# Graph attention and dilated SAGE: scores in sixteen 32x32 array tiles, and running counts over pairs of columns

## The chip, the core and the metric

The kernel runs on one core of one Trainium2 chip. The time is that of the device in microseconds (us), from one launch; before the change the median of 3 runs is 3443.05 us (3439.62 to 3444.79). In the profile, PE is TensorE's matmuls, PEld its weight loads, DVE is VectorE, ACT ScalarE, POOL GpSimd and SP the engine that starts most DMAs.

## What is computed

The input is `x` (16 graphs of 1024 nodes with 128 features) and a weighted adjacency `adj` (16 x 1024 x 1024). There are two layers, each on a layer-normed, rectified `x`, each added to `x`. The first is attention with 8 heads of 16 features, masked by the edges and weighted by them:

```python
scores = einsum('bhnd,bhmd->bhnm', q, k) / math.sqrt(HD)
scores = where(adj == 0, -inf, scores)
attn = softmax(scores) * adj
attn = attn / (attn.sum(-1) + 1e-08)
ctx = einsum('bhnm,bhmd->bhnd', attn, v)      # then @ Wo.T + bo
```

The second first "dilates" the edges, node by node, since what an earlier node removes changes the counts of the later ones:

```python
row = carry[n]; num = sum(row)
sf = where(num > 10, (num + 1) // 2, 1)
rank = cumsum(row)
rm = row & (rank % sf == 0)                   # if valid and num > 1
carry[n] = row & ~rm; carry[:, n] = carry[:, n] & ~rm
```

With what is left of `adj`, three SAGE layers follow (neighbour means, two products, normalised rows, batch norm), and one product of all three.

## The kernel before

All lines are those of the profile. The work has two parts in time. In the first, attention runs over `turns` (L180): 16 graphs b, 2 halves c of the query nodes, 8 blocks m of 128 key nodes, and in each turn two groups g of four heads. That is 512 attention steps. Beside them, in the same instruction streams, runs the dilation, over 8 blocks k of 128 nodes for all 16 graphs at once. In the second part the SAGE layers run.

The order on TensorE, ScalarE and VectorE is the order in which the program is written out (the schedule is manual for these three engines, L1197). An attention step (L572 to L608) issues: the scores of its group; small pieces of other graphs' preparation; the value products of the step before (`late`); two exps on ScalarE (L590); two multiplications by the edge weights on VectorE (L595). Every second step also turns over a block of edges (`turn_over`, L489): four transposes, a copy, and the mask of missing edges, `nomask`, which is kept in four versions, version r rotated by 32r partitions (L507 to L509).

`scores` (L531) fills four PSUM banks, one for each head j of the group, held as two tiles `scs` of two banks each. First, 16 bfloat16 matmuls (L546) put -1e30 where an edge is missing; each uses one 32x32 tile of the array, and for one j the four row strips r all write bank j, in four different quarters of its partitions. Then four float32 matmuls (L552), one for each head, add the scores: 32 rows (the group's head j lies in row strip j, the other heads of the strip being zeroed in `qT`) by all 128 columns. The exps read the two tiles of `scs`, and the next step's scores are written to the same four banks.

`values` (L476) multiplies the weights by `v1`, 32 columns for each head: 16 values, a one (for the sum of the weights) and 15 zeros, in 128x32 array tiles (L479); with `eps8` it adds 1e-8 of the plain softmax sum (L484). The two buffers of `v1` for alternate graphs share one tile under the tag `aT2`.

The dilation of a block (`dilation`, L643) is a generator whose yields give an estimated cost and when it may go on: 0 at once, 1 in the next attention step, "A" or "B" in the next even or odd one. `beside_attention` (L936) takes pieces from it while the estimated cost spent is below the share of steps done. For a block it first finds which nodes of the block remove each other: counts inside the block (`w`, scanned at L747, shifted by 1024 and masked by `valid` at L785), seven rounds of comparing and counting (L799 to L841), and the block's final counts. Then come the block's rows, graph by graph (L889 to L933): a running sum along the row of 1024 nodes. The scan at L893 adds each node's edge and that of the node before, so that it yields the doubled count less a shift; ScalarE takes the absolute distance to a middle (`mid_at`, L906); VectorE compares it with `off` and keeps the edges to be removed (L910 to L915); eight transposes turn it (L900), ScalarE copies it (L902), and DMAs write both. In the same loop ScalarE reads the next block's edges (`read`, L691 and L695) and VectorE drops those already removed (`survive`, L708).

Of the kernel before, what the change touches and what calls it, by code (L numbers as in the profile page):

```python
# [10 lines left out]
F32 = mybir.dt.float32  # L11
# [10 lines left out]
P = 128  # L22
# [12 lines left out]
def swept(ctx: ExitStack, tc: tile.TileContext, t: dict, out: bass.AP, flag: bass.AP):  # L35
# [131 lines left out]
    def first_part(p1):  # L167
# [73 lines left out]

        v1_both = shared.tile([P, 2, NB, H, 32], F32, name="v1_both", tag="aT2")
        v1s = [v1_both[:, i] for i in range(2)]
        for v1 in v1s:
            nc.vector.memset(v1[:, :, :, HD:], 0.0)
            nc.vector.memset(v1[:, :, :, HD : HD + 1], 1.0)
        never = one.tile([P, P], BF, name="never")
# [37 lines left out]
        def prepare(b):  # L285
# [35 lines left out]
            def value(c, bank=(ps_m, "m")):  # L321
                pv = bank[0].tile([P, HB, D], F32, name=f"pv_{b}_{c}", tag=bank[1])
                start_with(pv, 0)
                for i in range(HB):
                    n = (c * HB + i) * P
                    nc.tensor.matmul(
                        pv[:, i, :], hT[:, n : n + P], wts["Wv"], start=False, stop=(i == HB - 1)
                    )
                yield "evict"
                nc.scalar.copy(  # L330
                    v1[:, c * HB : (c + 1) * HB, :, :HD], pv.rearrange("p k (h d) -> p k h d", d=HD)
                )
# [139 lines left out]
        def attention():  # L472
# [3 lines left out]
            def values(acc, v1, m, g, es, ws):  # L476

                for j in range(4):
                    nc.tensor.matmul(  # L479
                        acc[g][32 * j : 32 * j + 32, :], v1[:, m, 2 * j + g, :],  # L480
                        ws[j // 2][:, j % 2, :], start=(m == 0), stop=False,
# [49 lines left out]
            def scores(i, g):  # L531
# [5 lines left out]
                nomask = tiles[i][1]  # L537
                mm = slice(m * P, (m + 1) * P)
                scs = [
                    ps_s.tile([P, 2, HN], F32, name=f"sc_{b}_{c}_{m}_{g}_{q}", tag="sc")  # L540
                    for q in range(2)
                ]
                for j in range(4):
                    for r in range(4):
                        rows, to = slice(32 * r, 32 * r + 32), 32 * ((r + j) % 4)
                        nc.tensor.matmul(  # L546
                            scs[j // 2][to : to + 32, j % 2, :], never[rows, rows], nomask[rows, j, :],
                            start=True, stop=False, tile_position=(32 * r, to),
                        )
                for j in range(4):  # L550
                    rows = slice(32 * j, 32 * j + 32)
                    nc.tensor.matmul(  # L552
                        scs[j // 2][:, j % 2, :], kT[rows, mm], qTs[c][rows, g, :],
                        start=False, stop=True, tile_position=(32 * j, 0),
                    )
                made["of"], made["scores"] = (i, g), scs
# [86 lines left out]
        def dilation():  # L643
# [84 lines left out]
            for k in range(NB):  # L728
# [5 lines left out]

                up = shared.tile([P, B, P], BF, name=f"up_{k}", tag="mr", bufs=4)

# [3 lines left out]
                for dg, hb in zip(dgs, halves):  # L740
                    nc.vector.tensor_tensor(up[:, hb, :], dg, each_half(upto), ALU.mult)
                next(late, None)
                yield 1.3, 1
# [16 lines left out]
                for c, hb in enumerate(halves):  # L760
# [3 lines left out]
                    if c == 0:  # L764
                        nc.vector.tensor_copy(onw, w[:, :, P - 1])
                        for dg, of in zip(dgs, halves):
# [17 lines left out]

                nc.vector.scalar_tensor_tensor(  # L785
                    w.rearrange("p b i -> p (b i)"), w.rearrange("p b i -> p (b i)"), 1024.0,
                    valid.rearrange("p b i -> p (b i)"), ALU.add, ALU.mult,
                )
                yield 2.3, 1
                final = shared.tile([P, B, P], BF, name=f"final_{k}", tag="mr", bufs=4)  # L790
# [53 lines left out]

                th = small.tile([P, 4, B], F32, name=f"th_{k}", tag="th", bufs=2)
                num, mid_at, off, allof = (th[:, i, :] for i in range(4))
                high = v[:, 3, :]
# [7 lines left out]
                nc.vector.tensor_scalar(num, num, MAGIC, MAGIC, ALU.add, ALU.subtract)  # L855
                nc.vector.tensor_scalar(mid_at, num, -3.0, 1024.0, ALU.mult, ALU.add)
                nc.vector.scalar_tensor_tensor(off, num, 1.0, high, ALU.add, ALU.mult)
# [31 lines left out]
                for i in range(B + 2):  # L889
                    b = i  # L890
                    if b < B:
                        wrs[b] = pool.tile([P, N], F16, name=f"wr_{k}_{b}", tag="wr", bufs=2)
                        nc.vector.tensor_tensor_scan(  # L893
                            wrs[b], rk(b, 1, N + 1), rk(b, 2, N + 2), -1023.0, ALU.add, ALU.add
                        )
                    b = i - 2
                    if 0 <= b:
# [4 lines left out]
                        nc.scalar.copy(ets[b], pe)  # L902
                    yield (2.4 if i < B else 0.0), "B"
                    b = i
                    if b < B:
                        nc.scalar.activation(wrs[b], wrs[b], AF.Abs, bias=mid_at[:, b : b + 1])  # L906
                    b = i - 1
# [28 lines left out]
        def beside_attention():  # L936

            block = 1.3 + 4.6 + 3.9 + 1.4 + 1.2 + 3.6 + ROUNDS * 2.5 + 2.0 + 5.1 + 1.4 + B * 5.3 + 2.4
            total = B * 0.3 + NB * block
# [1023 lines left out]
```

## Time and profile before

| what | value |
|---|---|
| median of 3 runs | 3443.05 us |
| the profiled execution, its own time | 3445.77 us |
| its span, first to last instruction | 3443.9 us |
| mean granted TensorE clock | 0.994 |
| the first part (attention and dilation) ends at | about 2355 us |
| matmuls in 0 to 2355 us | 25771 |
| exps (L590) | 1024 x 1020 ns |
| edge multiplications (L595) | 1024 x 1217 ns |
| scans of rows (L893) | 128 x 2278 ns |

A row of the profile's groups reads: line, engine, operation, output <- inputs, partitions x elements and type of each, count | busy time in us, mean ns of one | idle time of the engine just before, and what ended it. Times by stage give, for each stretch of the span, its length, then the busy time of each engine with its number of instructions, the granted clock, the share of DMA and its rate. A timeline row gives the start, the time covered, the engine, the line and how many instructions are merged in it.

### The profile page before, as it was taken

How to read it: one execution, taken by the hardware profiler on the slowest of the kernel's cores; microseconds unless marked ns; L12 is line 12 of the kernel's file. 1: busy time of each engine (PE TensorE's matmuls, PEld its weight loads, DVE VectorE, ACT ScalarE, POOL GpSimd, SP SyncE). 2: the span in 40 equal slices, each digit the busy share in tenths (PEclk: the TensorE clock that was granted, in tenths of full speed). 3: DMA queues.
4: the chain of work that ended last, by engine and by line, in shares of the span. 5: the costliest groups of instructions: out<-in, count | busy, mean ns of one | idle time of the engine just before them, and what ended most of it. 6: DMA issues, size and time to landing. Idle time of an engine off the chain costs nothing. (4 is left out here: it accounts for less than half of the span.)

```text
span 3443.9 us, 86074 instructions
## 1 busy us (share of the span) xinstructions
PE 3364.4 (98%) x34855; PEld 1882.4 (55%) x34855; DVE 3096.0 (90%) x5255; ACT 2287.3 (66%) x3781; POOL 174.4 (5%) x253
## 2 busy tenths in 40 slices
PE   8999999999999999999999999999999899999997
PEld 3333333333333333333334334336999899999997
DVE  7899999889989999998998999997888799988887
ACT  7699689779879869968876986884322344423234
POOL 2000000000000000000000000000000000000000
PEclk9999999999999999999999999999999999999999
DMA  7356457547637746745763773677999799989996
GB/s 238 107 171 197 137 148 200 153 129 222 187 117 213 213 124 182 227 142 157 228 191 121 229 236 120 185 218 248 345 334 337 271 354 353 350 309 350 356 352 222
DMA packets 650121, 772.27 MB, mean 224 GB/s; under 512 B 173264, under 2 KB 569168, under 8 KB 637424
## 3 DMA queue, kind: packets, MB, share of 16 engines
q1 hardware_dynamic: 632672, 708.58, 63.7%
q0 software_dynamic: 15456, 57.30, 4.9%
q8 instruction: 275, 4.51, 0.6%
q14 instruction: 134, 1.10, 0.1%
q10 hardware_dynamic: 1584, 0.79, 0.1%
HBM read 508.50 MB, written 157.29 MB: 193 GB/s over the span
## 5 line engine op out<-in xcount | busy, mean ns | idle before, releaser
L595 DVE TENSOR_TENSOR w<-e,aT 128x1024 f32<-128x1024 f32 x1024 | 1203.9, 1217 | 107.9 <-ACT e L590 107.4
L590 ACT ACTIVATE e<-sc 128x1024 f32<-128x1024 f32 x1024 | 990.4, 1020 | 341.7 <-PE sc L552 340.6
L1117 PE MATMUL pg<-y,aT 128*128 128x128 f32 (+1 forms) x6144 | 732.2, 275 | 0.0
L1117 PEld LDWEIGHTS pg<-y,aT 128*128 128x128 f32 x6144 | 710.3, 192 | 0.0
L479 PE MATMUL acc<-w,v_both 128*32 128x512 f32 x4096 | 637.2, 605 | 6.9 <-DVE w L595 3.8
L484 PE MATMUL acc<-e,eps 128*32 128x512 f32 x4096 | 617.3, 593 | 0.0
L552 PE MATMUL sc<-qT,kT 32*128 32x512 f32 x4096 | 584.3, 640 | 0.3 <-ACT qT L308 0.3
L146 DVE SCALAR_TENSOR_TENSOR aT<-mr,aT 128x1024 f32<-128x1024 bf16 x384 | 458.8, 1217 | 0.0
L484 PEld LDWEIGHTS acc<-e,eps 128*32 128x32 f32 x4096 | 159.1, 110 | 294.6 <-issue 286.0
L1140 ACT ACTIVATE sq<-o 128x512 f32<-128x512 f32 x96 | 60.6, 631 | 358.1 <-DVE o L1135 358.1
L893 DVE TENSOR_TENSOR_SCAN wr<-rk 128x1024 f16<-128x1024 bf16 x128 | 291.6, 2278 | 0.0
L546 PEld LDWEIGHTS <-never 32*32 32x32 bf16 x8192 | 79.1, 88 | 340.4 <-issue 317.6
L546 PE MATMUL sc<-nomask,never 32*32 32x512 bf16 x8192 | 249.2, 385 | 11.0 <-ACT e L590 7.5
L1158 ACT COPY hT<-pt 128x512 f32<-128x512 f32 x96 | 56.2, 585 | 267.7 <-PE pt L1154 259.3
L552 PEld LDWEIGHTS sc<-qT,kT 32*128 32x128 f32 x4096 | 160.1, 183 | 116.9 <-issue 116.1
L479 PEld LDWEIGHTS acc<-w,v_both 128*32 128x32 f32 x4096 | 100.7, 108 | 203.6 <-DVE w L595 105.0
L497 PEld LDWEIGHTS pa<-ident,a 128*128 128x128 f32 x1024 | 108.1, 141 | 181.7 <-issue 134.2
L906 ACT ACTIVATE wr<-wr,th 128x1024 f16<-128x1024 f16 x128 | 148.0, 1156 | 46.8 <-DVE wr L893 45.8
L497 PE MATMUL pa<-ident,a 128*128 128x128 f32 x1024 | 168.8, 288 | 6.8 <-DMA a<-in_adj 6.1
L504 ACT ACTIVATE nomask<-aT 128x512 bf16<-128x512 f32 x256 | 161.4, 630 | 8.1
L1135 DVE SCALAR_TENSOR_TENSOR o<-pg,rdeg,mine 128x128 f32<-128x128 f32 x384 | 108.1, 344 | 60.4 <-PE pg L1117 56.8
L500 ACT COPY aT<-pa 128x512 f32<-128x512 f32 x256 | 151.6, 592 | 4.7 <-PE pa L497 4.7
(226 smaller groups left out, 3844.5 us busy)
## 6 DMA issues: line engine op xcount, KB each, us to landing
aT<-aT_d SPq DMA_DIRECT2D x94, 2048.0 KB, 9.8
mr<-mr_d SPq DMA_DIRECT2D x188, 512.0 KB, 6.1
aT_d<-aT SPq DMA_DIRECT2D x256, 256.0 KB, 4.1
a<-in_adj SPq DMA_DIRECT2D x253, 256.0 KB, 4.1
ad<-in_adj SPq DMA_DIRECT2D x112, 512.0 KB, 4.2
nomask<-nomask SPq DMA_DIRECT2D x512, 96.0 KB, 2.7
nomask<-nomask SPq DMA_DIRECT2D x512, 64.0 KB, 2.7
nomask<-nomask SPq DMA_DIRECT2D x512, 32.0 KB, 2.8
```

What stands on the lines that cost most here:

```text
L146: nc.vector.scalar_tensor_tensor(part, mrs[h][:, j : j + 2, :].rearrange("p j n -> p (j n)"), 0.0, part, ALU.is_equal, ALU.mult)
L479: nc.tensor.matmul(acc[g][32 * j : 32 * j + 32, :], v1[:, m, 2 * j + g, :], ws[j // 2][:, j % 2, :], start=(m == 0), stop=False,)
L484: nc.tensor.matmul(acc[g][32 * j : 32 * j + 32, :], eps8, es[j // 2][:, j % 2, :], start=False, stop=(m == NB - 1),)
L497: nc.tensor.transpose(pa[:, k * P : (k + 1) * P], a[:, k, :], ident)
L500: nc.scalar.copy(aT[:, 0, :], pa)
L504: nc.scalar.activation(nomask[:, 0, :], aT[:, 0, :], AF.Relu, bias=1.0, scale=-1e38, accum_out=zeros[:, i : i + 1])
L546: nc.tensor.matmul(scs[j // 2][to : to + 32, j % 2, :], never[rows, rows], nomask[rows, j, :], start=True, stop=False, tile_position=(32 * ...
L552: nc.tensor.matmul(scs[j // 2][:, j % 2, :], kT[rows, mm], qTs[c][rows, g, :], start=False, stop=True, tile_position=(32 * j, 0),)
L590: nc.scalar.activation(e, scs[q], AF.Exp, scale=1.0 / math.sqrt(HD))
L595: nc.vector.tensor_tensor(w, es[q], aT.to_broadcast([P, 2, HN]), ALU.mult)
L893: nc.vector.tensor_tensor_scan(wrs[b], rk(b, 1, N + 1), rk(b, 2, N + 2), -1023.0, ALU.add, ALU.add)
L1117: nc.tensor.matmul(pg[:, i // 2, at : at + width], aT[:, j, i * P : (i + 1) * P], y[:, j, :width], start=(j == 0), stop=(j == NB - 1),)
```

## The change

It has two halves.

The scores: a group's four float32 products become sixteen, each in a 32x32 tile of the array: head j stays in row strip j, and its 128 key columns go to four column tiles. The loops run with the rotation q outside and the row strip j inside, and row strip j writes column tile (q + j) mod 4 of bank j. The masks are rewritten in the same order, so that a row strip's mask goes to its own bank.

The counts: the scan of a row runs over 513 pairs of neighbouring columns in place of 1024 columns, and gives the plain count at the end of each pair, in float16. ScalarE then makes both columns of a pair from it, with a scale of 2 and two biases, writing every second element: from sum i for the even column and from sum i + 1 for the odd. The two buffers of pair sums lie in the tile of the value weights, which now stand 17 apart for each head (the 32 columns of a load run into the next head's; the rows of `acc` that come of it are not read). In the block's own counts, 1024 is put into the first column before the scan, so the later step is a multiplication alone. The estimated costs of the pieces are set to match.

```diff
-        v1_both = shared.tile([P, 2, NB, H, 32], F32, name="v1_both", tag="aT2")
-        v1s = [v1_both[:, i] for i in range(2)]
+        HW = HD + 1
+        VW = H * HW + 16
+        both = shared.tile([P, 4096], F32, name="both", tag="aT2")
+        v1s = [both[:, i * NB * VW : (i + 1) * NB * VW].rearrange("p (m w) -> p m w", w=VW) for i in range(2)]
...
+        free = 2 * NB * VW
+        pair_sums = [
+            both[:, free + i * (HN // 2 + 1) : free + (i + 1) * (HN // 2 + 1)].bitcast(F16)[:, : HN + 1]
+            for i in range(2)
+        ]
...
-                        acc[g][32 * j : 32 * j + 32, :], v1[:, m, 2 * j + g, :],
+                        acc[g][32 * j : 32 * j + 32, :], v1[:, m, (2 * j + g) * HW : (2 * j + g) * HW + 32],
...
-                for j in range(4):
-                    for r in range(4):
-                        rows, to = slice(32 * r, 32 * r + 32), 32 * ((r + j) % 4)
+                for q in range(4):
+                    for j in range(4):
+                        rows, to = slice(32 * j, 32 * j + 32), 32 * ((q + j) % 4)
                         nc.tensor.matmul(
-                            scs[j // 2][to : to + 32, j % 2, :], never[rows, rows], nomask[rows, j, :],
-                            start=True, stop=False, tile_position=(32 * r, to),
+                            scs[j // 2][to : to + 32, j % 2, :], never[rows, rows], nomask[rows, q, :],
+                            start=True, stop=False, tile_position=(32 * j, to),
                         )
-                for j in range(4):
-                    rows = slice(32 * j, 32 * j + 32)
-                    nc.tensor.matmul(
-                        scs[j // 2][:, j % 2, :], kT[rows, mm], qTs[c][rows, g, :],
-                        start=False, stop=True, tile_position=(32 * j, 0),
-                    )
+                for q in range(4):
+                    for j in range(4):
+                        rows, to = slice(32 * j, 32 * j + 32), 32 * ((q + j) % 4)
+                        nc.tensor.matmul(
+                            scs[j // 2][to : to + 32, j % 2, :],
+                            kT[rows, m * P + to : m * P + to + 32], qTs[c][rows, g, :],
+                            start=False, stop=True, tile_position=(32 * j, to),
+                        )
...
-                up = shared.tile([P, B, P], BF, name=f"up_{k}", tag="mr", bufs=4)
+                up = shared.tile([P, B, P], F16, name=f"up_{k}", tag="mr", bufs=4)
...
+                nc.vector.tensor_scalar(up[:, :, 0:1], up[:, :, 0:1], 1024.0, None, ALU.add)
...
-                nc.vector.scalar_tensor_tensor(
-                    w.rearrange("p b i -> p (b i)"), w.rearrange("p b i -> p (b i)"), 1024.0,
-                    valid.rearrange("p b i -> p (b i)"), ALU.add, ALU.mult,
-                )
-                yield 2.3, 1
+                nc.vector.tensor_tensor(w, w, valid, ALU.mult)
+                yield 1.3, 1
...
-                nc.vector.tensor_scalar(mid_at, num, -3.0, 1024.0, ALU.mult, ALU.add)
+                nc.vector.tensor_scalar(at_odd, num, -3.0, None, ALU.mult)
+                nc.vector.tensor_scalar(at_even, num, -3.0, 2.0, ALU.mult, ALU.add)
...
-                        wrs[b] = pool.tile([P, N], F16, name=f"wr_{k}_{b}", tag="wr", bufs=2)
+                        row = rk(b, 0, N + 2)
                         nc.vector.tensor_tensor_scan(
-                            wrs[b], rk(b, 1, N + 1), rk(b, 2, N + 2), -1023.0, ALU.add, ALU.add
+                            pair_sums[b % 2], row[:, 0::2], row[:, 1::2], 0.0, ALU.add, ALU.add
                         )
...
-                    yield (2.4 if i < B else 0.0), "B"
+                    yield (1.3 if i < B else 0.0), "B"
...
-                        nc.scalar.activation(wrs[b], wrs[b], AF.Abs, bias=mid_at[:, b : b + 1])
+                        wrs[b] = pool.tile([P, N], F16, name=f"wr_{k}_{b}", tag="wr", bufs=2)
+                        for t, at in enumerate((at_even, at_odd)):
+                            nc.scalar.activation(
+                                wrs[b][:, t::2], pair_sums[b % 2][:, t : t + HN], AF.Abs,
+                                bias=at[:, b : b + 1], scale=2.0,
+                            )
...
-            block = 1.3 + 4.6 + 3.9 + 1.4 + 1.2 + 3.6 + ROUNDS * 2.5 + 2.0 + 5.1 + 1.4 + B * 5.3 + 2.4
+            block = 1.3 + 4.6 + 3.9 + 1.4 + 1.2 + 2.6 + ROUNDS * 2.5 + 2.0 + 5.1 + 1.4 + B * 4.2 + 2.4
```

More of the change, by code (lines that the diff above doesn't have):

```diff
@@ L239, in node_masks @@
             )
-        v1_both = shared.tile([P, 2, NB, H, 32], F32, name="v1_both", tag="aT2")
-        v1s = [v1_both[:, i] for i in range(2)]
+        HW = HD + 1
+        VW = H * HW + 16
+        both = shared.tile([P, 4096], F32, name="both", tag="aT2")
+        v1s = [both[:, i * NB * VW : (i + 1) * NB * VW].rearrange("p (m w) -> p m w", w=VW) for i in range(2)]
         for v1 in v1s:
-            nc.vector.memset(v1[:, :, :, HD:], 0.0)
-            nc.vector.memset(v1[:, :, :, HD : HD + 1], 1.0)
+            nc.vector.memset(v1[:, :, H * HW :], 0.0)
+            nc.vector.memset(v1[:, :, HD : H * HW : HW], 1.0)
+        free = 2 * NB * VW
[3 more added lines that the diff above has]
+        ]
         never = one.tile([P, P], BF, name="never")
@@ L330, in value @@
                 nc.scalar.copy(
-                    v1[:, c * HB : (c + 1) * HB, :, :HD], pv.rearrange("p k (h d) -> p k h d", d=HD)
+                    v1[:, c * HB : (c + 1) * HB, : H * HW].rearrange("p k (h e) -> p k h e", e=HW)[:, :, :, :HD],
+                    pv.rearrange("p k (h d) -> p k h d", d=HD),
                 )
@@ L537, in scores @@
                 nomask = tiles[i][1]
-                mm = slice(m * P, (m + 1) * P)
                 scs = [
@@ L764, in dilation @@
                     if c == 0:
-                        nc.vector.tensor_copy(onw, w[:, :, P - 1])
+                        nc.vector.tensor_scalar(onw, w[:, :, P - 1], 1024.0, None, ALU.subtract)
                         for dg, of in zip(dgs, halves):
@@ L841, in dilation @@
                             nc.tensor.matmul(g, final[:, b, :], vb[:, 1, b, 0:1], start=False, stop=True)
-                th = small.tile([P, 4, B], F32, name=f"th_{k}", tag="th", bufs=2)
-                num, mid_at, off, allof = (th[:, i, :] for i in range(4))
+                th = small.tile([P, 5, B], F32, name=f"th_{k}", tag="th", bufs=2)
+                num, at_odd, off, allof, at_even = (th[:, i, :] for i in range(5))
                 high = v[:, 3, :]
```

## The prediction

> **What bounds the kernel now.** I read the page first, then busy time by stage, then the timeline of two attention steps, then the groups by form.
>
> The page's busy rows and its 40 slices:
>
> ```profile
> PE 3364.4 (98%) x34855; PEld 1882.4 (55%) x34855; DVE 3096.0 (90%) x5255; ACT 2287.3 (66%) x3781; POOL 174.4 (5%) x253
> ...
> PE   8999999999999999999999999999999899999997
> DVE  7899999889989999998998999997888799988887
> ACT  7699689779879869968876986884322344423234
> PEclk9999999999999999999999999999999999999999
> ```
>
> Attention with the dilation beside it fills some 27 slices (to about 2355 us, where the last L546 and L552 start); the SAGE layers fill the rest, and the change doesn't touch them. ScalarE's row swings in attention, eight times. So I cut that part at the first L893 scan of each block and 12 us after its last one: "row stages", where each block's 16 rows of counts are built (about 34 attention steps each), and "other stages" between them.
>
> ```profile
> core 0: us, PE busy (x) PEld busy (x) DVE busy (x) ACT busy (x) POOL busy (x), PEclk, DMA share, GB/s
> 177.51:325.58 148.07, 146.35 (x1574) 52.42 (x1574) 140.60 (x197) 143.25 (x234) 6.93 (x6) 1.00 0.64 183
> 325.58:453.15 127.57, 126.98 (x1526) 46.81 (x1510) 113.64 (x198) 90.72 (x142) 6.99 (x8) 1.00 0.46 140
> ...
> 1876.71:2038.55 161.84, 158.72 (x1589) 54.91 (x1580) 158.44 (x214) 142.68 (x207) 6.03 (x6) 1.00 0.77 225
> 2038.55:2169.45 130.90, 130.34 (x1683) 51.76 (x1667) 120.29 (x230) 89.72 (x136) 10.57 (x16) 1.00 0.47 142
> 2169.45:2317.07 147.62, 145.63 (x1580) 51.87 (x1576) 144.33 (x170) 125.69 (x170) 8.90 (x13) 1.00 0.69 207
> ```
>
> The other stages (second and fourth rows) are TensorE's: 99% busy, VectorE at 89 to 92%, ScalarE at 70%. The row stages are close to three bounds at once: in block 0 ScalarE is at 97%, VectorE at 95%; by block 6 VectorE is at 98% and ScalarE at 88%. All eight row stages last 148.07, 149.93, 151.63, 153.92, 157.00, 159.47, 161.84, 147.62; the last has no next block to read.
>
> A busy TensorE need not be at its peak, so I took the timeline of one step on it:
>
> ```profile
> 1001.88 0.43 PE L546 MATMUL sc<-nomask,never 32*32 32x512 bf16 x16
> 1002.25 1.14 PE L552 MATMUL sc<-qT,kT 32*128 32x512 f32 x8
> ...
> 1002.78 0.61 PE L552 MATMUL sc<-qT,kT 32*128 32x512 f32 x4
> 1003.32 0.66 PE L497 MATMUL pa<-ident,a 128*128 128x128 f32 x4
> 1003.91 1.07 PE L479 MATMUL acc<-w,v_both 128*32 128x512 f32 x8
> 1004.79 1.04 PE L484 MATMUL acc<-e,eps 128*32 128x512 f32 x8
> ```
>
> Each float32 product is two array passes (four products, eight instructions). L479 to L484 is 0.88: two passes of 0.43 and 0.03 for the first weights, with no seam, since both use 128x32 tiles. L552's first pass takes 0.53 (1002.25 to 1002.78), so 0.10 of it is the load of 128 weight columns; its second takes 0.54, so 0.11 is emptying the array before another shape. Masks and scores together: 0.37 + 1.07 = 1.44 us a step, 512 steps.
>
> **The scores.** Both groups now use 32x32 tiles. Gone are the emptying between L546 and L552 (0.11) and the exposed load (0.10): 32 columns load in 0.03 and can load while the masks stream. What stays: first load 0.03, mask pass 0.21 (an estimate: half of a float32 pass), two score passes 0.86, the spread of 16 starts 0.05 to 0.10, emptying 0.11. That is 1.26 to 1.31; I take 1.28, so 0.16 saved. From below: if the seam isn't a matter of shape, nothing is saved.
>
> It adds 24 matmuls and 24 weight loads a step. Row L546: 16 loads of 88 ns each cover 0.14 us, so starts are about 3.5 ns apart. Against the change speaks the Trainium skill, "TensorEngine Tiling (Array Packing)", section Instruction Overhead: about 60 cycles per matmul, which at the 2.4 GHz of its TensorE page is 25 ns. By it 24 more cost 0.6 us a step, 0.6 - 0.21 = +0.4 net. This trace has such a row too, but for full-array matmuls:
>
> ```profile
> 395.30 0.16 PE L840 MATMUL gone<-vb,valid 128*128 128x1 bf16 x1
> 395.33 0.16 PE L841 MATMUL gone<-vb,final 128*128 128x1 bf16 x1
> ```
>
> 25 ns apart, all in one array tile. L546 is the nearer row (same tiles, same 512 columns), and I go by it. Streaming four column tiles of float32 at once is L479's habit; four row strips at once is L552's.
>
> The same page (Gotcha 1) says that different row tiles can't use one PSUM bank at a time. Before, L546 wrote one bank from four row strips, in different quarters, and its 16 still took 0.37; after, each strip has its bank. By the rule the masks would gain; by the row they are already one pass. I count nothing.
>
> A wait moves: the first four masks now touch all four banks, so the first mask waits for both exps, where before eight masks went ahead of the second exp. Queued behind it on TensorE are all masks, the scores, then the previous step's values. But before, no score could start until the last eight masks had followed the second exp, so the exp-to-score distance is about one mask pass either way: 0 (at most +0.05).
>
> **The counts.** Rows by form:
>
> ```profile
> L893 DVE TENSOR_TENSOR_SCAN wr<-rk 128x1024 f16<-128x1024 bf16 x128 | 291.6, 2278 | 0.0
> L830 DVE TENSOR_TENSOR hit<-w,at 128x2048 bf16<-128x2048 f16 x56 | 68.2, 1218 | 0.5
> L785 DVE SCALAR_TENSOR_TENSOR w<-w,valid 128x2048 f16<-128x2048 f16 x8 | 18.2, 2274 | 0.0
> L504 ACT ACTIVATE nomask<-aT 128x512 bf16<-128x512 f32 x256 | 161.4, 630 | 8.1
> L906 ACT ACTIVATE wr<-wr,th 128x1024 f16<-128x1024 f16 x128 | 148.0, 1156 | 46.8 <-DVE wr L893 45.8
> ```
>
> - Scan: 2278 ns for 1024 steps is 2.22 ns a step; 513 steps are 1.14 us, up to 1.3 if the stride-2 reads cost. I take 1.17: 1.11 less a row, 17.8 a row stage, VectorE.
> - Abs: one pass over 1024 becomes two over 512. L504 is 630 for 512; a per-partition bias costs 0.1 (L906's 1156 against 1051 for L691's 1024 without one; L317's 512 with one takes 692). Two of 0.71, less the 0.10 by which the two exps of a step overlap (1.94 for two of 1.02), is 1.32 to 1.40: +0.16 to +0.25 (+0.3 if interleaved writes cost), I take 0.21, ScalarE: +3.4 a row stage.
> - L785 becomes a tensor_tensor of 2048 like L830: -1.05 a block; two added small VectorE instructions (175 ns, row L856) +0.35. This lies in the other stages, where VectorE waits anyway: 0; if VectorE were the bound there, -0.7 x 8 = -6.
> - The value weights at a stride of 17: the same 512 elements per copy (L330, 591 ns) and 32 columns per load: 0. The pair sums share a tile with them; if that made either wait for the other, the scan of row b+2 is a row (some 9 us) behind row b's Abs, and the value copy comes twice an image: 0, at worst 1 us an image.
> - The planner's costs shrink, but in the code a block has some 62 yields that demand a new attention step; 8 of them fill nearly all 512 steps. The dilation keeps its pace in steps: 0. No DMA, SP or POOL instruction is added or moved.
>
> **The sum.** Row stages, blocks 0 to 6: ScalarE's busy time is 143.25, 141.74, 144.31, 145.19, 145.09, 144.71, 142.68. VectorE falls to 123 to 141. TensorE needs at most the 145.6 of block 7's stage, which does the same work, less 34 x 0.16 = 5.4: 140. So ScalarE comes last. With 3.4 more each and 98% busy (block 0 has 97% with both others beside it), the stages take 149.6, 148.1, 150.7, 151.6, 151.5, 151.1, 149.1: 1051.7 against 1081.9, -30. Block 0's grows by 1.5. Block 7's, with ScalarE at 125.7 + 3.4 and VectorE at 126.6, follows TensorE: -5.5. Other stages: 512 - 8 x 34 = 240 steps x 0.16 = 38; VectorE, up from 90% to 93%, will hand some back (its L595 feeds L479), so nine tenths: -34. Total -69.5: 3445.8 of the profiled execution (its span 3443.9) becomes 3376; from the median 3443.05, 3374.
>
> **Rivals.**
> - *ScalarE takes more of it.* For: its 97% in block 0. With +0.3 per Abs and 96.7%: (1007.0 + 33.6)/0.967 = 1076, -6; other stages -25, block 7 -5: 3407. Beside it, *the seam stays* (the change doesn't do what it says on TensorE): only -30: 3413.
> - *Everything shrinks.* TensorE at 1.23 (0.2 saved, 240 steps: -48), ScalarE at 99.5% in row stages (-46), -7: 3342. Against: three engines would have to mesh better than now.
> - *Slower: TensorE can't start the pairs fast enough.* Behind the masks' wait for the second exp stand 16 + 32 load-and-matmul pairs. At L840's 25 ns the last pair starts at 1.20 and ends at 1.20 + 0.43 + 0.11 = 1.74, 0.30 over today. It decides from 48d + 0.54 = 1.44, d = 19 ns. Other stages +72; row stages 145.6 + 10.2 = 155.8 at 98.7%, 158 each, +35: 3550. For: that row and the skill's 60 cycles. Against: L546's 3.5 ns in these tiles.
>
> **Chances.** Likeliest 0.46 (3355 to 3395); everything shrinks 0.13; ScalarE 0.13; seam stays 0.06; gains and costs level out within 0.2%, about what a measurement of this kernel can tell from no change, 0.06; slower 0.16. Faster 0.78. The range goes from 3335 (the second case) over the level case to 3450, leaving out the slower one.
>
> **What would show it.** Right: from the first L546 to the group after L552 about 1.28 us in place of 1.44, with no gap between L546 and L552; L893 at 1.17 us; two L906 rows near 0.7 us; row stages near 150 us and level over the blocks, ScalarE 97 to 98% in them; other stages 4 to 5 us shorter. Wrong: score starts 25 ns apart, or second passes waiting for another column tile of their row strip (then five passes, 2.1 us); waits of L893 on TensorE, which would be the shared tile; a row stage that follows VectorE still.

## The result, and the profile after

The changed kernel takes 3462.15 us (median of 5 runs, 3457.27 to 3464.22) against 3442.01 for the kernel before beside it: ratio 1.0057, 95% interval 1.0042 to 1.0072. It is 0.6% slower, where 3374 was predicted. The profiled execution spans 3462.4 us, 18.5 more than before.

The page of the changed kernel, its busy row and two of its 40 slices:

```profile
PE 3360.8 (97%) x47143; PEld 1947.8 (56%) x47143; DVE 2968.8 (86%) x5271; ACT 2332.1 (67%) x3909; POOL 163.8 (5%) x253
...
DVE  7888988888889898988988999897888799988887
ACT  7699689779869968967976986894232344423334
```

VectorE lost 127 us of work, ScalarE gained 45, TensorE's busy time is nearly the same (3360.8 for 3364.4) with 12,288 more matmuls, and the span grew. So the work of the two fullest engines doesn't account for the new time; it has to be looked for in when things start. Busy time by stage of the changed kernel, cut as before (row stage and other stage of block 0; row stage 6, other stage, row stage 7):

```profile
core 0: us, PE busy (x) PEld busy (x) DVE busy (x) ACT busy (x) POOL busy (x), PEclk, DMA share, GB/s
176.18:326.58 150.40, 146.16 (x2326) 56.85 (x2326) 124.77 (x196) 148.65 (x250) 4.86 (x6) 1.00 0.61 178
326.58:458.06 131.48, 129.98 (x2250) 51.47 (x2246) 113.56 (x200) 91.32 (x142) 6.97 (x8) 1.00 0.47 140
1899.01:2051.64 152.63, 150.70 (x2353) 59.46 (x2333) 141.65 (x213) 146.94 (x222) 4.97 (x6) 1.00 0.76 227
2051.64:2190.71 139.07, 135.92 (x2410) 56.26 (x2403) 120.81 (x234) 90.50 (x137) 10.57 (x16) 1.00 0.49 148
2190.71:2335.63 144.92, 143.86 (x2384) 56.66 (x2368) 129.40 (x170) 131.65 (x186) 7.83 (x13) 1.00 0.71 214
```

The row stages look much as predicted: level at about 150 us, VectorE with room, ScalarE at 96 to 99% in the first seven. The eight last 150.4, 152.4, 151.2, 151.5, 152.9, 153.8, 152.6, 144.9, together 19.7 less than before, where 35.5 was predicted. The loss is in the other stages: 131.48 for 127.57, and 139.07 for 130.90. All other stages together, from 20 us to the last scores, went from 1103.9 to 1142.6, +38.7. The granted clock is 1.00 in all the stages shown, as before.

The groups of the changed kernel (same columns as before):

```profile
L604 DVE TENSOR_TENSOR w<-e,aT 128x1024 f32<-128x1024 f32 x1024 | 1206.3, 1219 | 219.7 <-ACT e L599 218.3
L560 PE MATMUL sc<-qT,kT 32*32 32x512 f32 x16384 | 703.5, 592 | 0.5 <-ACT qT L315 0.5
L553 PE MATMUL sc<-nomask,never 32*32 32x512 bf16 x8192 | 285.4, 384 | 38.1 <-ACT e L599 26.8
L916 ACT ACTIVATE wr<-both,th 128x512 f16<-128x512 f16 x256 | 206.3, 884 | 2.0 <-DVE both L901 1.6
L901 DVE TENSOR_TENSOR_SCAN both<-rk 128x513 f16<-128x513 bf16 x128 | 156.0, 1218 | 0.0
```

The scan fell as forecast (1218 ns for an expected 1170). The Abs did not: 884 ns for an expected 710. And one step on TensorE in the changed kernel's timeline:

```profile
1186.23 1.06 PE L487 MATMUL acc<-w,both 128*32 128x512 f32 x8
1187.11 1.04 PE L492 MATMUL acc<-e,eps 128*32 128x512 f32 x8
1188.09 0.62 PE L908 MATMUL pe<-ident_bf,er 128*128 128x128 bf16 x8
1188.64 0.43 PE L553 MATMUL sc<-nomask,never 32*32 32x512 bf16 x16
1188.86 1.34 PE L560 MATMUL sc<-qT,kT 32*32 32x512 f32 x32
1190.13 1.13 PE L322 MATMUL pk<-hT,attn_w 128*128 128x512 f32 x2
```

The masks last 0.22 (1188.64 to 1188.86) where they lasted 0.37: the emptying between masks and scores is gone, as predicted. But the scores last 1.27 (1188.86 to 1190.13) where they lasted 1.07. Medians over the steps in which nothing waits in between: from the first mask to the first score 365 ns before and 226 after, from there to the next group 1072 and 1272, together 1.437 and 1.498 us. A step is 0.06 us longer, not 0.16 shorter.

### The profile page after: what moved, and what is told of

Same layout as the page of the kernel before. It is cut to its first block, busy times and chain, and to the rows that moved or that the text cites. A ratio compares the mean times of both kernels' runs of the same rounds, so it can differ in the third digit from the quotient of the medians.

```text
span 3462.4 us, 110792 instructions
## 1 busy us (share of the span) xinstructions
PE 3360.8 (97%) x47143; PEld 1947.8 (56%) x47143; DVE 2968.8 (86%) x5271; ACT 2332.1 (67%) x3909; POOL 163.8 (5%) x253
## 5 line engine op out<-in xcount | busy, mean ns | idle before, releaser
L560 PE MATMUL sc<-qT,kT 32*32 32x512 f32 x16384 | 703.5, 592 | 0.5 <-ACT qT L315 0.5
L487 PE MATMUL acc<-w,both 128*32 128x512 f32 x4096 | 567.4, 605 | 6.7 <-DVE w L604 6.0
L492 PE MATMUL acc<-e,eps 128*32 128x512 f32 x4096 | 553.5, 592 | 0.0
L553 PE MATMUL sc<-nomask,never 32*32 32x512 bf16 x8192 | 285.4, 384 | 38.1 <-ACT e L599 26.8
L553 PEld LDWEIGHTS <-never 32*32 32x32 bf16 x8192 | 93.8, 87 | 390.1 <-issue 362.3
L492 PEld LDWEIGHTS acc<-e,eps 128*32 128x32 f32 x4096 | 141.6, 110 | 300.8 <-issue 296.5
L560 PEld LDWEIGHTS sc<-qT,kT 32*32 32x32 f32 x16384 | 275.4, 103 | 29.5 <-ACT qT L315 0.8
L916 ACT ACTIVATE wr<-both,th 128x512 f16<-128x512 f16 x256 | 206.3, 884 | 2.0 <-DVE both L901 1.6
L487 PEld LDWEIGHTS acc<-w,both 128*32 128x32 f32 x4096 | 86.5, 108 | 147.6 <-issue 60.9
L901 DVE TENSOR_TENSOR_SCAN both<-rk 128x513 f16<-128x513 bf16 x128 | 156.0, 1218 | 0.0
```

What stands on the lines that cost most here:

```text
L487: nc.tensor.matmul(acc[g][32 * j : 32 * j + 32, :], v1[:, m, (2 * j + g) * HW : (2 * j + g) * HW + 32], ws[j // 2][:, j % 2, :], start=(m ...
L492: nc.tensor.matmul(acc[g][32 * j : 32 * j + 32, :], eps8, es[j // 2][:, j % 2, :], start=False, stop=(m == NB - 1),)
L553: nc.tensor.matmul(scs[j // 2][to : to + 32, j % 2, :], never[rows, rows], nomask[rows, q, :], start=True, stop=False, tile_position=(32 * ...
L560: nc.tensor.matmul(scs[j // 2][to : to + 32, j % 2, :], kT[rows, m * P + to : m * P + to + 32], qTs[c][rows, g, :], start=False, stop=True ...
L901: nc.vector.tensor_tensor_scan(pair_sums[b % 2], row[:, 0::2], row[:, 1::2], 0.0, ALU.add, ALU.add)
L916: nc.scalar.activation(wrs[b][:, t::2], pair_sums[b % 2][:, t : t + HN], AF.Abs, bias=at[:, b : b + 1], scale=2.0,)
```

## The experiments

Two questions stood open: why the scores take 0.20 more, and whether that explains the time. My theory after the first reading: TensorE holds only a limited number of instructions ahead of time, so that part of the 16 tiles comes late. The rivals: the scores' slower starts are a price for each matmul (the prediction's slower case), or the masks' wait on both exps (the moved wait) holds up the step, or the new counts cost what the scores seem to.

Sums of the stages in the runs compared below, us (row stages; other stages from 20 us to the last scores), each from one profiled execution, so that a difference of a few us is not to be trusted by itself:

| kernel | row | other |
|---|---|---|
| before | 1229.5 | 1103.9 |
| changed | 1209.8 | 1142.6 |
| counts half alone | 1200.0 | 1103.2 |
| scores half alone | 1234.8 | 1120.1 |
| masks in strip order alone | 1229.0 | 1103.3 |
| changed without masks | 1185.3 | 1075.0 |
| counts half, scores in 32x64 tiles | 1202.4 | 1109.3 |
| counts half, copies of turned edges on VectorE | 1194.0 | 1115.4 |
| before, copies on GpSimd's queue | 1230.4 | 1109.4 |
| changed, copies on GpSimd's queue | 1210.7 | 1113.9 |
| changed, copies split | 1210.8 | 1109.8 |
| before, copies split | 1230.5 | 1103.4 |
| counts half, contiguous halves | 1196.4 | 1107.9 |
| the same, copies split | 1196.0 | 1099.8 |

**The two halves (counts, scores), and the moved wait (mask_order).** `counts` is the kernel before with all of the diff but the scores and masks; `scores` is the kernel before with only those. `mask_order` keeps the four wide products and only rewrites the masks' order:

```diff
-                for j in range(4):
-                    for r in range(4):
-                        rows, to = slice(32 * r, 32 * r + 32), 32 * ((r + j) % 4)
+                for q in range(4):
+                    for j in range(4):
+                        rows, to = slice(32 * j, 32 * j + 32), 32 * ((q + j) % 4)
...
-                            scs[j // 2][to : to + 32, j % 2, :], never[rows, rows], nomask[rows, j, :],
-                            start=True, stop=False, tile_position=(32 * r, to),
+                            scs[j // 2][to : to + 32, j % 2, :], never[rows, rows], nomask[rows, q, :],
+                            start=True, stop=False, tile_position=(32 * j, to),
```

> The change's counts alone (pair scan, two Abs, value weights 17 apart), with the masks and scores of before. Theory 1 (TensorE's queue costs the score half, ScalarE's two long Abs take back most of the count half): TensorE's masks and scores are back at 1.44 us a step, the other stages at 128 to 131 us, the row stages near 150 because ScalarE is at 97%: 8 x 150 = 1200 against 1229.5, so about -25 to -30: 3415, ratio 0.992. Theory 2 (the counts are what makes it slower, by the longer Abs or by the tile they share with the value weights): slower than before, 3450 to 3460.

> The change's masks and scores alone, with the counts of before. Theory 1: from the first mask to the next group 1.50 us in place of 1.44, so the other stages grow by 240 x 0.06 = 15 us plus what the moved wait costs, and the row stages grow too, since VectorE is still at 98% there: 3475 to 3490, ratio 1.010 to 1.014. Theory 2 (the counts are at fault): within 0.2% of before or faster, 3400 to 3445.

> Before, with only the order of the masks changed: each row strip writes its own bank, so the first masks wait for both exps; scores and counts are those of before. If the moved wait is dear (the part of the loss in the other stages that 0.06 us a step doesn't explain, some 20 us), this is slower by 10 to 20 us, 3455; if it costs nothing, as I predicted, within 0.2%. If one bank from four row strips held up the masks, the mask group gets shorter than 0.37 us.

Measured: counts 3413.33, ratio 0.9925 (0.9912 to 0.9938); scores 3463.55, 1.0063 (1.0050 to 1.0075); mask_order 3442.21, 1.0003 (0.9995 to 1.0011). So the counts gain 28 us, the scores lose 22, and the moved wait costs nothing, though masks wait in other places. The scores stayed below the 3475 to 3490 that was expected of them. The scores half's other stages grew by 16.2; some 248 steps there at 0.06 are 15. Its row stages grew by only 5.3, a third of what 264 steps would cost; that the fuller VectorE (95 to 98% busy there) hides the rest is argued, not shown. But -28 and +22 are -6, and the change costs +19 to +20: the halves don't add up. That was a second question.

**Why the scores are late (no_masks, interleaved).** `no_masks` is the changed kernel without the mask matmuls; `interleaved` puts each tile's mask directly ahead of its own score:

```diff
-                        nc.tensor.matmul(
-                            scs[j // 2][to : to + 32, j % 2, :], never[rows, rows], nomask[rows, q, :],
-                            start=True, stop=False, tile_position=(32 * j, to),
-                        )
...
-                            start=False, stop=True, tile_position=(32 * j, to),
+                            start=True, stop=True, tile_position=(32 * j, to),
```

```diff
                 for q in range(4):
                     for j in range(4):
                         rows, to = slice(32 * j, 32 * j + 32), 32 * ((q + j) % 4)
+                        at = scs[j // 2][to : to + 32, j % 2, :]
...
-                for q in range(4):
-                    for j in range(4):
-                        rows, to = slice(32 * j, 32 * j + 32), 32 * ((q + j) % 4)
...
```

> The change without its masks: the scores of missing edges are not put at -1e30, so the softmax runs over all pairs. Per step 32 instructions fewer stand ahead of the 64 of the scores. Theory 1 (64 instructions at a time): all or nearly all 16 first passes start within about 0.11 us of each other (at most the last three or four late), in place of eight at once and eight from 0.19 to 0.30 us. Rival (only eight float32 tiles run at once, or TensorE starts a tile each 16 ns): the second eight still start 0.19 to 0.30 us late.

> The change with each tile's mask directly ahead of its own score instead of all masks first: the same instructions in another order. Theory 1 (64 instructions are held, and places come free in order): 64 are ten tiles of six and four of the eleventh; the next tiles must wait for the first tile's second pass, about 1.1 us, and TensorE needs 2.3 to 2.6 us from the first mask to the next group in place of 1.50: 3900 to 4000. Rival (starting a tile costs 16 ns, in whatever order): 1.4 to 1.6 us, 3440 to 3480.

Measured: 3372.18 and 3860.97, one run each. The first time says little, since the masks' own work is gone from it. But inside one score group the start times tell the cause. Each float32 product is two passes with a weight load each, so a tile is four instructions, and a step holds 16 x 2 for masks and 16 x 4 for scores, 96. Busy time of the scores alone in six stretches of the changed kernel's group above; the count in brackets is of matmuls running in the stretch:

```profile
core 0: us, PE busy (x) PEld busy (x), PEclk, DMA share, GB/s
1188.84:1188.94 0.10, 0.08 (x8) 0.10 (x9) 1.00 0.70 154
1188.94:1189.04 0.10, 0.10 (x8) 0.05 (x8) 1.00 0.85 184
1189.04:1189.18 0.14, 0.14 (x16) 0.13 (x14) 1.00 0.54 172
1189.18:1189.28 0.10, 0.10 (x16) 0.10 (x13) 1.00 0.86 230
1189.28:1189.38 0.10, 0.10 (x24) 0.01 (x1) 1.00 1.00 282
```

Eight tiles run at once, and for 0.18 us no ninth joins them. Over all steps the first eight start 0 to 23 ns after the first, 3.4 ns apart; the other eight at 186, 203, 219 and so on to 303, 16.7 apart. The second passes follow in two groups as well, from 429 and from 614, the last at 754; before, the last second pass started at 553. These 0.20 us are the whole loss of the scores. The same view of the run without masks:

```profile
core 0: us, PE busy (x) PEld busy (x), PEclk, DMA share, GB/s
1184.86:1184.96 0.10, 0.09 (x14) 0.09 (x24) 1.00 0.04 10
1184.96:1185.06 0.10, 0.10 (x16) 0.10 (x32) 1.00 0.00 0
```

Now 14 run within the first 0.1 us and all 16 within 0.2: the same tiles, the same weights, only 32 instructions fewer ahead of them. Eight tiles of four and 32 for the masks are 64; 16 tiles of four are 64. And the timeline of the interleaved order, where a tile is six:

```profile
1184.13 0.48 PE L554 MATMUL sc<-nomask,never 32*32 32x512 bf16 x11
1184.35 1.12 PE L558 MATMUL sc<-qT,kT 32*32 32x512 f32 x22
1184.97 0.37 PE L554 MATMUL sc<-nomask,never 32*32 32x512 bf16 x1
1185.39 0.58 PE L558 MATMUL sc<-qT,kT 32*32 32x512 f32 x1
1185.41 0.46 PE L554 MATMUL sc<-nomask,never 32*32 32x512 bf16 x4
```

Eleven masks go out at once: ten tiles of six are 60, and the first four instructions of the eleventh make 64. The twelfth mask comes only at 1184.97, some 0.03 us after the record of the first tile's first score pass ends (it starts at 1184.35; such a record is 0.59 long); the group takes 2.5 us. In the changed kernel the ninth tile, too, starts some 0.03 after the first mask's record ends (0.41 and 0.38 after the first mask's start). Three orders, three counts, one limit: about 64 instructions are held ahead, and what lies behind them starts as earlier ones end. Loads and matmuls come in pairs in all three, so a limit of 32 pairs would look the same. The Trainium skill states this figure (TensorE: Matmul & The Clock Gate, the table at its head: an engine queue 64 deep for TensorE); these runs agree. A fixed price of 25 or 16 ns for each tile falls: starts are 3.4 ns apart in the changed kernel while all is held, and 14 of the 16 tiles without masks start 6.7 apart.

**Fewer instructions (counts_64).** The counts half, with the scores in eight 32x64 tiles: 32 + 32 instructions.

```diff
-                for j in range(4):
-                    rows = slice(32 * j, 32 * j + 32)
-                    nc.tensor.matmul(
-                        scs[j // 2][:, j % 2, :], kT[rows, mm], qTs[c][rows, g, :],
-                        start=False, stop=True, tile_position=(32 * j, 0),
-                    )
+                for h in range(2):
+                    for j in range(4):
+                        rows, to = slice(32 * j, 32 * j + 32), 64 * ((h + j) % 2)
+                        nc.tensor.matmul(
+                            scs[j // 2][to : to + 64, j % 2, :],
+                            kT[rows, m * P + to : m * P + to + 64], qTs[c][rows, g, :],
+                            start=False, stop=True, tile_position=(32 * j, to),
+                        )
```

> The counts half with the scores in eight 32x64 tiles: 32 instructions, which with the 32 of the masks are 64. Theory 1: no tile starts late (eight starts within about 0.06 us); the emptying between the two shapes is back (0.37 for the masks), the exposed load is 64 columns (0.05): 0.37 + 0.05 + 0.85 + 0.05 + 0.09 = 1.41 us from the first mask to the next group, 0.02 less than before; 3405 to 3414, the same as the counts alone or just better. Rival (each further tile costs time by itself): more than 1.44 us, slower than 3414.

Measured: 3424.73, ratio 0.9939 (0.9926 to 0.9952). The group is 0.03 shorter than before the change (1.410: the first passes start 6.7 ns apart with no break, which fits the limit of 64; but the 365 ns from masks to scores are back, with tiles of two shapes again). The time missed the expected 3405 to 3414: the shorter group didn't shorten it, and by the ratios it can't be told from the counts half alone (0.9925). The other stages are 6.1 longer than there, for a reason that the next runs bear on but don't settle for this kernel.

**The Abs (counts_halves), and ScalarE's load (counts_et).** To the counts half: the two Abs write contiguous halves and the comparison interleaves them; and, for `counts_et`, VectorE copies every second graph's turned edges in blocks 0 to 5.

```diff
-                                wrs[b][:, t::2], pair_sums[b % 2][:, t : t + HN], AF.Abs,
+                                wrs[b][:, t * HN : (t + 1) * HN], pair_sums[b % 2][:, t : t + HN], AF.Abs,
...
-                            er, wrs.pop(b), off[:, b : b + 1], allof[:, b : b + 1], ALU.is_equal, ALU.max
+                            er.rearrange("p (i t) -> p i t", t=2), wrs.pop(b).rearrange("p (t i) -> p i t", t=2),
+                            off[:, b : b + 1], allof[:, b : b + 1], ALU.is_equal, ALU.max
```

```diff
-                        nc.scalar.copy(ets[b], pe)
+                        (nc.vector.tensor_copy if b % 2 and k < 6 else nc.scalar.copy)(ets[b], pe)
```

> The counts half alone, but each Abs writes one contiguous half of the row in place of every second element; VectorE's comparison reads the two halves interleaved instead. If the interleaved write makes the Abs long (884 ns where I took 710), they fall to 690 to 740 ns; if it is the bias and the scale, they stay near 880. VectorE's comparison grows from 537 ns to 0.6 to 1.1 us. ScalarE's busy time in a row stage falls by about 16 x 0.3 = 5 us; the row stages by 2 to 4 us each in blocks 0 to 4: 3395 to 3405 against 3413 of the counts alone. If the writes are not it: 3413 to 3425.

> The counts half with the copies of the turned rows of every second graph moved from ScalarE to VectorE in blocks 0 to 5. Theory 1 (ScalarE, 97 to 99% busy, ends the row stages of the counts half): ScalarE falls by 8 x 1.0 us a stage, VectorE rises by 8 x 0.7; the stages of blocks 0 to 5 fall from 150 to 153 to about 147, then held by TensorE: -15 to -25, 3390 to 3400. Rival (TensorE or the chain from exp to score holds the row stages already): within 0.2% of 3413.

Measured: 3407.85, 0.9884 (0.9868 to 0.9899); 3417.34, 0.9921 (0.9908 to 0.9934). The group of the counts half, then two of the version with contiguous halves:

```profile
L915 ACT ACTIVATE wr<-both,th 128x512 f16<-128x512 f16 x256 | 205.0, 879 | 1.8 <-DVE both L900 1.7
```

```profile
L915 ACT ACTIVATE wr<-both,th 128x512 f16<-128x512 f16 x256 | 172.2, 732 | 5.6 <-DVE both L900 5.3
L922 DVE TENSOR_SCALAR er<-wr,th 128x1024 bf16<-128x1024 f16 x128 | 102.8, 803 | 0.0
```

732 is about what the prediction took (0.71); the interleaved write of 2-byte values is the other 147 ns. Reading the two halves alternately has a price on VectorE: the comparison went from 537 to 803. Both times missed what was expected (3395 to 3405; 3390 to 3400). The second is what its rival foresaw, that TensorE or the chain from exp to score holds the row stages already. Busy time in the first seven row stages, us:

| kernel | length | ScalarE | TensorE | VectorE |
|---|---|---|---|---|
| before | 1081.8 | 1007.0 | 1065.2 | 1050.3 |
| changed | 1064.8 | 1038.2 | 1035.8 | 937.4 |
| counts half alone | 1056.9 | 1038.7 | 1024.4 | 939.8 |
| counts half, contiguous halves | 1052.7 | 1017.5 | 1027.3 | 965.8 |
| counts half, copies of turned edges on VectorE | 1051.0 | 1006.6 | 1029.2 | 960.3 |

With the counts half alone ScalarE is 98.3% busy, and comes last. But 21 us less of its work, or 32 less (the copy takes 667 ns on VectorE against 992 on ScalarE), shorten these stages by only 4 and 6: TensorE is then at 98% and stands next. In `counts_et` the other stages give it back: 1115.4, +12.2.

**Where the rest went (changed_pool, before_pool, halves_pool, counts_et_pool).** The waits of TensorE of the kernel before, then of the changed kernel (total us, times, longest):

```profile
PE sc L546 <- ACT e L590: 7.5, 17, 0.5
...
PE sc L546 <- DMA nomask<-nomask: 2.5, 5, 0.7
```

```profile
PE sc L553 <- ACT e L599: 26.8, 66, 0.5
...
PE sc L553 <- DMA nomask<-nomask: 9.6, 20, 1.3
```

The first of these isn't the moved wait (8.4 us in `mask_order`, 7.2 in `scores`, which both have it). It came with the counts; in `counts`, with the masks in their old order, it reads:

```profile
PE sc L554 <- ACT e L598: 30.9, 77, 0.5
```

The second has grown: a rotated copy of the masks isn't there yet. The timeline of one of these places:

```profile
1770.38 0.59 SPq L516 DMA_DIRECT2D nomask<-nomask  x1
...
1771.02 1.31 SPq L517 DMA_DIRECT2D nomask<-nomask  x1
...
1771.03 0.39 PE L553 MATMUL sc<-nomask,never 32*32 32x512 bf16 x4
...
1772.43 1.84 PE L553 MATMUL sc<-nomask,never 32*32 32x512 bf16 x12 [1.00 <-DMA nomask<-nomask]
```

SP starts the last copy just as the first four masks run, which need none of them; TensorE then stands idle for 1.00 us before the other 12, and with them everything behind them on TensorE. Counting the distance between two starts wherever a mask waits over 40 ns for a copy, masks stand still for 12 us before, 11 in the counts half, 16 in the scores half, 23 in the counts half with contiguous halves, 29 in `counts_et` and 43 in the changed kernel. SP starts some 14 DMAs in two steps, about 0.5 us each, six of them these copies; it is 76% busy in row stages. It starts other loads too, and VectorE waits for one of them, `gl` (the edges already removed), 18.1 us in the changed kernel; before it was 2.9, and 6.4 and 8.3 in the halves:

```profile
L717 DVE SCALAR_TENSOR_TENSOR rk<-rk,gl 128x128 bf16<-128x128 bf16 (+6 forms) x112 | 76.8, 686 | 18.1 <-DMA gl<-mr_d 18.1
```

So four kernels were also run with the copies on GpSimd's queue:

```diff
-                    nc.sync.dma_start(nomask[: P - 32 * r, r, :], nomask[32 * r :, 0, :])
-                    nc.sync.dma_start(nomask[P - 32 * r :, r, :], nomask[: 32 * r, 0, :])
+                    nc.gpsimd.dma_start(nomask[: P - 32 * r, r, :], nomask[32 * r :, 0, :])
+                    nc.gpsimd.dma_start(nomask[P - 32 * r :, r, :], nomask[: 32 * r, 0, :])
```

> The change, with the six rotated copies of each mask tile started from POOL's queue in place of SP's. In the changed kernel the second to fourth versions of the masks held up TensorE for 38 us in all (before: 11), and the two halves of the change together lose some 27 us more than each alone. Theory 1 (SP's queue, 80% busy in the row stages, brings the copies late once TensorE is slower): the copies come in time, those stalls fall below 10 us, and the time falls by 20 to 30 us, to 3430 to 3440. Rival (the interaction is TensorE against ScalarE, the exps waiting for later scores): the stalls go but the time stays within 0.2% of 3462.

> The kernel before, with the mask copies started from POOL's queue: the control of changed_pool. If SP's queue is the only place where the two halves of the change met, this falls only by the 11 us for which late copies held up the masks before, to 3428 to 3436, and stands within 0.3% of changed_pool (3433): then the change itself, freed of that queue, is worth -28 + 22 = -6 us. If it falls by as much as the changed kernel did (29 us, to 3415), the queue was no interaction and the halves do not add up for another reason.

> What looked best: the counts half with contiguous Abs halves, scores as before, mask copies from POOL's queue. Counts with halves gave 3408; late copies held up its masks for 19 us, which go if theory 1 holds: 3385 to 3395, ratio 0.983 to 0.986. If the stalls only move to the exps: within 0.2% of 3408.

> counts_et with the mask copies from POOL's queue. counts_et took 6 us from the row stages and lost 12 in the other stages, where late copies held up the masks for 27 us in place of 19 or so. If that is where the relief of ScalarE went: 3385 to 3395. If ScalarE never ended the row stages: 3400 to 3407, the counts alone less 10 us.

Measured: changed 3433.19, 0.9967 (0.9954 to 0.9980); before 3448.22, 1.0015 (1.0008 to 1.0022); contiguous halves 3409.06, 0.9906 (0.9892 to 0.9919); copies of turned edges on VectorE 3406.37, 0.9894 (0.9879 to 0.9909). The stalls on copies are gone in all four. The changed kernel gains 29 us, `counts_et` 11; the contiguous halves gain nothing, where 3385 to 3395 was expected; the kernel before loses 6: its first stage grew from 157.5 to 163.1 us, and its other stages didn't shrink. So stalls of 12 to 23 us cost nothing that this move gives back, and those of 43 us cost much.

**Copies split (before_late, changed_late, halves_late).** To leave the start alone, the copies go to GpSimd's queue only from the twentieth turn on:

```diff
+                queue = nc.gpsimd if i >= 20 else nc.sync
...
-                    nc.sync.dma_start(nomask[: P - 32 * r, r, :], nomask[32 * r :, 0, :])
-                    nc.sync.dma_start(nomask[P - 32 * r :, r, :], nomask[: 32 * r, 0, :])
+                    queue.dma_start(nomask[: P - 32 * r, r, :], nomask[32 * r :, 0, :])
+                    queue.dma_start(nomask[P - 32 * r :, r, :], nomask[: 32 * r, 0, :])
```

> The kernel before, with the rotated mask copies started from GpSimd's queue from the twentieth turn on and from SP's before. All of them on GpSimd's queue took away the 11 us that masks waited for copies, but made the first stage some 5 us longer, and the time was 3448. If it was the start that cost, this runs in 3432 to 3440. If GpSimd's queue is no better than SP's for these copies, it stays at 3442 or above.

> The changed kernel, with the same split of the copies. If the lateness of copies and the start are all that hid it, the two halves add up to -6 beside the kernel before with the same split: 3425 to 3432 here. If the halves get into each other's way on an engine as well, the distance is nil or positive.

> The counts half alone with contiguous halves of the rows, and the same split of the copies: the version that beats both. Expected 3395 to 3403, ratio 0.987 to 0.989. If the copies cost this version nothing, 3408 as without the split.

Measured on one chip: before 3439.23, ratio 0.9998 (0.9989 to 1.0006); changed 3429.36, 0.9963 (0.9951 to 0.9976); contiguous halves 3403.98, 0.9894 (0.9879 to 0.9909). The first shows no gain: the kernel before had been losing nothing to its 12 us of late copies. The change is now 10 us faster than the kernel before with the same split, close to the sum of its halves (-6). The only wait of masks left in the changed kernel:

```profile
PE sc L554 <- ACT e L600: 28.7, 71, 0.5
```

The last came out just above its expectation; by the ratios the copies cost this version nothing either (0.9884 and 0.9894, with overlapping intervals). The counts half with contiguous halves is 1.1% below the kernel before and, by the two ratios, 1.6% below the changed one; only `counts_et_pool` (0.9894) is as fast.

## Why the prediction was wrong

**The step that failed** is "the spread of 16 starts 0.05 to 0.10", a term of the 1.28 us of a step. It multiplied the number of starts by a distance taken from 16 pairs (L546's 3.5 ns), and nothing was asked about 48 pairs in a row. 3.5 was right up to about the 64th instruction. Behind it the eight remaining tiles start 186 to 303 ns late, and of the second passes the first starts at 429 ns and the last at 754: a spread of 0.325. The other terms held. From the first mask to the first score 0.226 was measured (0.24 predicted); the first tile's second pass follows 429 ns after its first, where 533 lay between before (0.43 predicted, without the exposed load); from the last second pass to the next group 0.518 (0.54 predicted). With the spread these make 1.498, so both savings came, 0.14 and 0.10, and the spread took 0.30 for them. The slower rival had the right place and the wrong shape. Its formula, 48d + 0.54, gives 1.498 at d = 20 ns, just past its deciding 19; but no start is dearer by itself, and the 25 ns of L840 and of the skill's 60 cycles were both far off for this tile size (3.4 ns held, 16.7 for a tile of four instructions refilled).

**Other stages: -34 predicted, +38.7 measured.** With the copies split, so that none is late, the other stages are only 6.4 longer than those of the kernel before with the same split (1109.8 to 1103.4; 248 steps at 0.06 would be 15). From -34 to +6.4 is the scores' error, 40. The remaining 33 (1142.6 to 1109.8) go when the copies leave SP's queue.

**"No DMA, SP or POOL instruction is added or moved"** was true and not enough: the order stayed and the reserve went. I had not looked at SP's queue at all. In the changed kernel nine in ten turns have their edges' store, which stands directly ahead of the copies, started within 7.4 us of the edges being ready, against 4.8 before, 5.1 with the counts half and 5.6 with the scores half. That the queue's lateness is worth 33 us is shown by moving the copies. How much of it is the copies' own is not: in `changed_late` VectorE no longer waits for `gl` either. Why SP falls further behind with both halves than with either is not settled: its busy share is the same (0.74 to 0.77 in row stages, 0.57 to 0.59 in the others).

**The counts.** The scan was right within 0.05 us. The Abs pair costs +0.45 a row in place of +0.21, because an interleaved write was counted at nothing ("+0.3 if interleaved writes cost" stood at the edge, and was too small too). By rows that would be 3.8 us more on ScalarE in a row stage; of all its work together, the busy time rose by 4.5 a stage in the first seven, where 3.4 was predicted. Those stages gave 17 of the 30 us predicted, and block 7's 2.7 of 5.5. Most of what is missing isn't the Abs: with the counts alone the first seven gave 25 and block 7's 4.6. So of the 16 us missing in the eight row stages, 10 came with the scores, which were to relieve TensorE there and didn't; contiguous halves bring back 3.6. The rival "ScalarE takes more of it" was right about the Abs and wrong about its price: it left 6 us of gain in the first seven.

**What held.** The moved wait is free, and a bank for each row strip gains nothing (`mask_order`, 1.0003). With the counts alone ScalarE does come last in the row stages, at 98.3% for the 98 taken, but only by a few us before TensorE. The shared tile makes nobody wait (L901's idle time is 0.0), the value products at a stride of 17 still take 605 ns, and the planner's costs changed no pace: 32 or 33 steps a row stage before and after (34 was taken).

In sum: -69.5 predicted and +18.5 in the span is a miss of 88: 16 in the row stages (10 with the scores, most of the rest the Abs), about 40 in the other stages by the scores' starts, about 33 by SP's queue.

## What to carry to other kernels

Before splitting a matmul into more array tiles, count the instructions of the group, loads and matmuls, two of each for a float32 product, together with what stands ahead of them, against what TensorE holds (here 96 against 64). When an engine is made the bound, ask how far behind it the next one stands, before its work is made cheaper. When a change shortens or shifts a step, look at the queue that feeds it, too, even if it gets no new instruction. When two halves of a change don't add up, run them apart and ask what they share; here the half worth keeping was the plain one.

## What was not expected of the hardware

- TensorE runs ahead by about 64 instructions, shown by 8, 16 and 11 tiles at once for 32 + 64, 64 and 6 a tile. What stands behind them waits until about the end of an earlier one's record: the ninth tile of scores starts 0.41 us after the first mask, whose record is 0.38 long.
- Writing every second 2-byte element took ScalarE 879 ns in place of 732 (512 elements). Reading 2-byte elements alternately from two halves took VectorE 803 in place of 537 (1024).
- Starting the copies from GpSimd's queue made the first stage 5.6 us longer in the kernel before; from the twentieth turn on it cost nothing.
